# A graph attention and feed-forward kernel: three halves of the first product moved behind a branch, a longer ring of one-hots, and twelve one-hots formed by ScalarE

## The chip, the cores and the metric

The kernel runs on one core of one Trainium2 chip. The metric is device time in microseconds (us) of one execution; all times below are in us unless marked ns. The core's engines work side by side, each through its own queue of instructions in order, and wait for one another by semaphores: TensorE (PE in the profile; its weight loads are PEld), VectorE (DVE), ScalarE (ACT), GpSimd (POOL) and SyncE (SP), which here mostly issues DMAs.

## What is computed

1250 nodes carry 768 features each; 21250 directed edges (source, destination) join them, sorted by destination. The reference, cut to what matters here, is two layers of graph attention, and a feed-forward part with a few routed tokens behind them:

```
def gat_layer(x, W, att_src, att_dst, bias, src, dst, heads, out_ch, concat):
    h = (x @ W.T).reshape(n, heads, out_ch)
    a_src = jnp.einsum('nhc,hc->nh', h, att_src)
    a_dst = jnp.einsum('nhc,hc->nh', h, att_dst)
    e = jax.nn.leaky_relu(a_src[src] + a_dst[dst], NEG_SLOPE)
    m = jax.ops.segment_max(e, dst, num_segments=n)
    ex = jnp.exp(e - m[dst])
    denom = jax.ops.segment_sum(ex, dst, num_segments=n)
    alpha = ex / (denom[dst] + EPS)
    out = jax.ops.segment_sum(alpha[:, :, None] * h[src], dst, num_segments=n)
...
x = x + _L0_gnn_ref(_layernorm(x), edge_index, W1, ..., b2)   # 8 heads of 128, then 1 of 768
x = x + _L0_ffn_ref(_layernorm(x)[None], ...)[0]
```

## The kernel before

The kernel makes the sparse graph dense. Nodes are taken in 10 blocks of 125. A table `ct` holds for each pair (source, destination) how many edges join them; attention then becomes dense arithmetic on tables of 125 sources by 1250 destinations and products on TensorE.

**Counting the edges (to about 101 us).** The edges come in 170 chunks of 125, 17 to a block of destinations. For each chunk, `hot_chunk` (line 263) makes two tables of zeros and ones with one row per edge: `at` (which of a block's 125 sources; `places`, line 258, makes those of eleven chunks at once on VectorE, GpSimd makes those of the other six singly, line 276) and `by`, 420 wide (which of 42 destinations, times 10 blocks of sources). `by` is made by one VectorE instruction, line 241, into one of 12 places of `ring`: it is 1 where the column's number equals the edge's `key`. `count_chunk` (line 284) multiplies the two on TensorE and adds up in PSUM banks, one for each area of 50 destinations, three banks in turn. When an area is complete, ScalarE copies it to `ct` and to `staged` (lines 309 and 314); when a block of destinations is complete, TensorE turns it (line 322) and ScalarE makes `absent` of it (line 323), a table that is huge where no edge is.

**Between and behind the count.** `h1_half` (line 495) computes a half of h for one block of nodes and one of two groups of heads: 6 matmuls in fp32, which the profile records as 12, and a copy from PSUM by ScalarE (line 395). There are 40 such halves, in the list `fill`. Six are put between the chunks of the last three blocks, 20 directly behind the count (line 684), 2 and 4 behind the branch (lines 701 and 708), and the last eight between the steps of heads 0 and 1. `top_of_block` (line 610 in its body) is a VectorE instruction that finds, for one head and one block of destinations, the largest source value among the neighbours. Heads 0 to 3 are done ahead of the branch except for the last block.

**The branch (line 689).** If some edge does not fit its chunk's window, `count_all` counts anew; it is never taken with these inputs. All engines read the number of such edges (line 686) and pass the branch each in its own place: the `issue_after` above it puts the read behind the halves issued so far. Behind it, VectorE finishes the tops of the last block. `load_destination_rows` (line 615) then turns head 0's tops into rows: a small transpose on TensorE (`r_h_p`, line 576), a copy on VectorE, a DMA to DRAM (`r_h_d`) and one back that spreads the rows over all partitions (`rows_h`, line 625).

**The heads.** For each of 8 heads and each of 10 blocks of sources, `weights` forms a table `pt` of 125 by 1250: VectorE (line 634, which needs `rows_h`), ScalarE's exponential (line 637), VectorE again (line 638). TensorE multiplies it with h and adds up in `acc` (line 851). Three `pt` buffers turn. Tops of later heads (line 610), remaining halves, and from head 4 parts of the second layer's product (line 802) stand between the steps. Then follow the second layer (line 1015) and the feed-forward part.

The order on each engine is set by a scheduler at build time, from the order of the source and the `issue_after` hints, so the order of the lines is not that of the queues.

Of the kernel before, what the change touches and what calls it, by code (L numbers as in the profile page):

```python
# [26 lines left out]
BF16 = mybir.dt.bfloat16  # L27
F16 = mybir.dt.float16
I32 = mybir.dt.int32
U16 = mybir.dt.uint16  # L30
AF = mybir.ActivationFunctionType
# [4 lines left out]
D = 768  # L36
# [6 lines left out]
B = 125  # L43
NB = N // B
EC = E // B
# [9 lines left out]
WIN = 42  # L55
SB = N // B
# [16 lines left out]
def gnn_ffn(  # L73
# [25 lines left out]
    nc = tc.nc  # L99

    def pool(name, bufs=1, space=None, stack=ctx):
        if space is None:
            return stack.enter_context(tc.tile_pool(name=name, bufs=bufs, reuse_waits="tile"))
        return stack.enter_context(tc.tile_pool(name=name, bufs=bufs, space=space))
# [28 lines left out]
    ep = pool("early", stack=early)  # L133
# [5 lines left out]
    def ps_count(name):  # L139
        return psum_a.tile([128, 512], F32, tag="count", bufs=3, name=name)  # L140

    src_i = ep.tile([B, EC], I32, name="src_i")
    dst_i = ep.tile([B, EC], I32, name="dst_i")
    nc.sync.dma_start(src_i, src)
    nc.sync.dma_start(dst_i, dst)

    HW = NB * (C1 + 1)
    x4 = big.tile([128, 4 * HW], F32, tag="ga", name="x4")
    x6 = big.tile([128, 4 * HW], F32, tag="gb", name="x6")
    x_in = [x4[:B, b * D : (b + 1) * D] for b in range(4)]  # L150
    x_in += [x6[:B, b * D : (b + 1) * D] for b in range(6)]

# [18 lines left out]
    for i in range(2):  # L171
# [3 lines left out]
    node = ep.tile([B, N], F16, name="node")  # L175
    nc.gpsimd.iota(
        node, pattern=[[1, N]], base=0, channel_multiplier=0, allow_small_or_imprecise_dtypes=True
# [23 lines left out]
    key = ep.tile([B, EC], F32, name="key")  # L201
# [23 lines left out]
    ones = ep.tile([B, 1], F32, name="ones")  # L225
# [14 lines left out]
    def one_hot(t, col, nodes):  # L240
        return nc.vector.tensor_scalar(t, nodes, col, None, op0=OP.is_equal)  # L241
# [1 line left out]

    ring = ep.tile([B, 12, SB * WIN], BF16, name="ring")
    newest = {}

    AT_ONCE = 11
# [2 lines left out]
    def places_at_once(b, r0, r1):  # L252
        n = r1 - r0
        t = ep.tile([B, AT_ONCE, B], BF16, tag="places", bufs=2, name=f"places{b}_{r0}")
        for r in range(r0, r1):
            at_once[b * CPB + r] = t[:, r - r0]
        c = b * CPB + r0
        nc.vector.tensor_tensor(  # L258
            t[:, :n], node[:, :B].unsqueeze(1).to_broadcast([B, n, B]),
            place16[:, c : c + n].unsqueeze(2).to_broadcast([B, n, B]), OP.is_equal,  # L260
        )

    def hot_chunk(c):

        b, r = divmod(c, CPB)
        if r < AT_ONCE and c not in at_once:
            if b > 0:
                places_at_once(b, 0, AT_ONCE)
            else:
                places_at_once(b, r, min(AT_ONCE, r + 6))  # L270
        by = ring[:, c % 12]
        newest["of"] = one_hot(by, key[:, c : c + 1], node[:, : SB * WIN])
        if r < AT_ONCE:
            return at_once[c], by
        at = ep.tile([B, B], BF16, tag="at", bufs=12, name=f"at{c}")
        nc.gpsimd.tensor_scalar(at, node[:, :B], place[:, c : c + 1], None, op0=OP.is_equal)  # L276
        return at, by

# [5 lines left out]
    def count_chunk(c):  # L284
        at, by = hot_chunk(c)
        f = window_of(c)
        for k in areas_of[c]:
            first = k not in banks
            if first:
                banks[k] = ps_count(f"count{k}")  # L290
            d0, d1 = max(f, AREA * k), min(f + WIN, AREA * (k + 1))
            last = c == EC - 1 or k not in areas_of[c + 1]
            newest["count"] = nc.tensor.matmul(  # L293
                banks[k][:B, SB * (d0 - AREA * k) : SB * (d1 - AREA * k)], at,
                by[:, SB * (d0 - f) : SB * (d1 - f)],
                start=first, stop=last, skip_group_check=True,
            )
            if last:
                use_area(k)
# [355 lines left out]
    def first_tops(blocks, hs=range(EARLY)):  # L655
        for b in blocks:
            for h in hs:
                top_of_block(heads[h], b)
# [6 lines left out]
    def fill_behind(what, n):  # L665
        with tc.issue_after(newest[what].ins):
            for _ in range(n):
                fill.pop(0)()

    for b in range(3, NB):  # L670
# [10 lines left out]
            attention_columns()  # L681
            as1_lo, as1_hi = low_high(a1[:, 0], [B, H1, NB], "as1")
        first_tops(behind.get(b, ()), range(4))
    fill_behind("count", 20)
    with tc.issue_after(newest["h1"].ins):
        n_val = nc.values_load(n_i[:1, :1], min_val=0, max_val=E)
    first_tops(range(4, NB - 1), range(4))
# [17 lines left out]
    for h in (4, 5):  # L705
        load_source_row(heads[h], ap, as1_d[h], f"h{h}")
    first_tops(range(4, NB), [4])
    for _ in range(4):
        fill.pop(0)()
    load_source_row(heads[6], ap, as1_d[6], "h6")  # L710
    tops = []
# [293 lines left out]
    for q in range(NB // 2):  # L1005
        pt = pt2[q]
        for i in range(2):
# [14 lines left out]
            for g in (1, 0):  # L1022
                c = slice(g * 384, (g + 1) * 384)
# [4 lines left out]
        c = slice(2 * q, 2 * q + 2)  # L1028
# [158 lines left out]
    for r in range(2):  # L1187
        for g in range(2):
            q = 32 * (2 * (1 - r) + g)
            c = slice(g * 384, (g + 1) * 384)  # L1190
# [67 lines left out]
```

## Time and profile before

| | us |
|---|---|
| median of 3 runs | 757.32 (755.39 to 758.07) |
| the profiled execution | 756.6 |
| its span in the trace | 754.8 |
| TensorE busy | 707.8 (94%) |
| VectorE busy | 555.8 (74%) |
| ScalarE busy | 286.8 (38%) |
| GpSimd busy | 89.5 (12%) |

"Busy" is the time in which an engine executes, without waits that the profile can see; the share is an average over stages with different limits. The page's second part cuts the span into 40 slices of 18.9 us, each digit a busy share in tenths:

```profile
PE   4899899996999877899999999999999999999998
DVE  7969999679999999999999891579686422342313
ACT  5986441114364745655555565004253000010000
```

The first five slices are the count, the next three and a half the halves of h around the branch, then come the heads to slice 25, the second layer to slice 35, and the feed-forward part. VectorE is full from slice 8 to slice 22 and TensorE nearly everywhere; which of the two ends a stage is told by the waits and by the chain that ended last.

### The profile page before, as it was taken

What the parts mean: (1) busy time and instruction counts of PE and PEld (TensorE: products, weight loads), DVE (VectorE), ACT (ScalarE), POOL (GpSimd) and SP (SyncE); (2) the same over time, 40 slices, a digit from 0 to 9 for tenths busy, and PEclk for the clock granted to TensorE, in tenths of its full rate; (3) what the DMA queues carried; (4) which work ended last, traced back from release to release, by engine and by line L of the source; (5) the groups of instructions that cost most, each with busy time, mean ns of one, the idle gap of its engine ahead of it and who ended that gap; (6) DMA issues with size and microseconds to landing.
All of it is one profiled execution on the core that took longest, in us unless ns stands there. A gap on an engine that the chain in (4) does not pass through costs nothing.

```text
span 754.8 us, 10416 instructions
## 1 busy us (share of the span) xinstructions
PE 707.8 (94%) x4136; PEld 541.3 (72%) x4136; DVE 555.8 (74%) x956; ACT 286.8 (38%) x500; POOL 89.5 (12%) x95
## 2 busy tenths in 40 slices
PE   4899899996999877899999999999999999999998
PEld 3767788885999767888887886555555555676755
DVE  7969999679999999999999891579686422342313
ACT  5986441114364745655555565004253000010000
POOL 8357300000000000000000000100011011023110
PEclk9799999997999999999999999999999999999999
DMA  8444000333003220222220200321101010194811
GB/s 229 160 170 172 0 1 1 119 100 106 2 1 104 84 70 1 69 84 70 83 72 1 69 1 24 136 69 38 48 21 42 20 42 20 34 309 132 310 42 42
DMA packets 21702, 58.42 MB, mean 77 GB/s; under 512 B 2414, under 2 KB 7906, under 8 KB 20498
## 3 DMA queue, kind: packets, MB, share of 16 engines
q1 hardware_dynamic: 21598, 57.68, 23.1%
q8 instruction: 33, 0.54, 0.3%
q14 instruction: 19, 0.16, 0.1%
q10 hardware_dynamic: 52, 0.04, 0.0%
HBM read 53.74 MB, written 3.98 MB: 76 GB/s over the span
## 4 chain that ended last, share of the span: by engine, by line
PE 65%; DVE 25%; DMA 4%; issue 4%; ACT 2%; SPq 0%; DVEq 0%; ACTq 0%
PE acc L1015 16%; PE h2p L802 13%; PE acc L851 10%; DVE pt L634 9%; PE h1p L499 8%; DVE pt L638 6%; PE f L1080 5%; PE f L1064 5%; DVE unused L610 5%; DVE ring L241 2%; PE count L293 2%; DMA rows_h<-r_h_d 2%; DMA x<-in_x 2%; PE xt2p L391 1%; DVE st L381 1%
## 5 line engine op out<-in xcount | busy, mean ns | idle before, releaser
L851 PE MATMUL acc<-g,pt 125*125 125x129 f32 x1600 | 191.9, 278 | 23.5 <-DVE pt L638 23.3
L851 PEld LDWEIGHTS acc<-g,pt 125*125 125x125 f32 x1600 | 186.3, 191 | 36.3 <-DVE pt L638 30.8
L637 ACT ACTIVATE pt<-pt,as_lo 125x1250 f32<-125x1250 f32 (+1 forms) x130 | 128.0, 1012 | 174.9 <-DVE pt L634 173.8
L638 DVE SCALAR_TENSOR_TENSOR pt<-pt,ct 125x1250 f32<-125x1250 f32 (+1 forms) x130 | 133.0, 1050 | 5.2 <-ACT pt L637 5.0
L1015 PE MATMUL acc<-h,pt 125*125 125x385 f32 (+1 forms) x400 | 129.7, 486 | 0.0
L634 DVE SCALAR_TENSOR_TENSOR pt<-rows_h,as_hi 125x1250 f32<-125x1250 f32 x80 | 118.9, 1509 | 5.8 <-DMA rows_h<-r_h_d 4.7
L1015 PEld LDWEIGHTS acc<-h,pt 125*125 125x125 f32 x400 | 74.6, 187 | 53.9
L802 PE MATMUL h2p<-w2s,g 128*125 128x384 f32 x320 | 109.0, 488 | 0.1
L499 PE MATMUL h1p<-w1s,xt 128*125 128x256 f32 x480 | 108.5, 382 | 0.5 <-ACT g L395 0.5
L499 PEld LDWEIGHTS h1p<-w1s,xt 128*125 128x125 f32 x480 | 89.3, 189 | 13.6 <-ACT g L395 0.9
L802 PEld LDWEIGHTS h2p<-w2s,g 128*125 128x125 f32 x320 | 57.7, 188 | 36.5 <-issue 0.8
L610 DVE CUSTOM_DVE_ANT_0 unused<-rows,absent 125x1250 bf16<-125x1250 f32 x40 | 58.3, 1458 | 10.0 <-ACTq L689 8.3
L1011 POOL TENSOR_TENSOR xb<-xb,b2r 125x768 f32<-125x768 f32 x10 | 18.3, 1832 | 372.3 <-DMA xb<-in_x 352.3
L610 DVE CUSTOM_DVE_ANT_0 unused<-srow_h,absent 125x1250 bf16<-125x1250 f32 x40 | 58.1, 1453 | 0.3
L276 POOL TENSOR_SCALAR at<-node,place 125x125 bf16<-125x125 f16 x60 | 49.5, 842 | 26.9 <-PE count L293 24.0
L241 DVE TENSOR_SCALAR ring<-node,key 125x420 bf16<-125x420 f16 x170 | 47.8, 344 | 6.3 <-PE count L293 6.2
L1084 DVE TENSOR_TENSOR o<-f,o 125x384 f32<-125x384 f32 x20 | 11.1, 557 | 52.5 <-PE f L1080 28.7
L293 PE MATMUL count<-ring,places 125*125 125x420 bf16 (+26 forms) x192 | 33.5, 303 | 16.0 <-DVE ring L241 15.6
L395 ACT ACTIVATE g<-h1p 125x256 f32<-125x256 f32 x40 | 15.3, 383 | 70.2 <-PE h1p L499 68.6
L293 PEld LDWEIGHTS <-places 125*125 125x125 bf16 x192 | 24.1, 154 | 21.8 <-DVE places L258 9.8
L1080 PE MATMUL f<-wf,gt 128*125 128x384 f32 x120 | 39.5, 486 | 0.0
L1080 PEld LDWEIGHTS f<-wf,gt 128*125 128x125 f32 x120 | 22.5, 188 | 15.1
(189 smaller groups left out, 579.5 us busy)
## 6 DMA issues: line engine op xcount, KB each, us to landing
rows_h<-r_h_d SPq DMA_DIRECT2D x8, 1250.0 KB
w_more<-in_atom_in_t SPq DMA_DIRECT2D x3, 1152.0 KB
w_more<-in_atom_out_t SPq DMA_DIRECT2D x3, 1152.0 KB
x<-in_x SPq DMA_DIRECT2D x10, 336.0 KB
xb<-in_x SPq DMA_DIRECT2D x10, 336.0 KB
srow_h<-as_d SPq DMA_DIRECT2D x5, 625.0 KB
w1n<-in_w SPq DMA_DIRECT2D x2, 1536.0 KB
w1s<-in_w1t SPq DMA_DIRECT2D x2, 1536.0 KB
```

The source lines that it names most:

```text
L241: return nc.vector.tensor_scalar(t, nodes, col, None, op0=OP.is_equal)
L276: nc.gpsimd.tensor_scalar(at, node[:, :B], place[:, c : c + 1], None, op0=OP.is_equal)
L293: newest["count"] = nc.tensor.matmul(banks[k][:B, SB * (d0 - AREA * k) : SB * (d1 - AREA * k)], at, by[:, SB * (d0 - f) : SB * (d1 - f)], ...
L499: newest["h1"] = nc.tensor.matmul(p[:B, :256], xt[:, k, b * B : (b + 1) * B], w1s[g][:, k, i * 256 : (i + 1) * 256], start=(k == 0), stop= ...
L610: nc.vector.tensor_tensor_reduce(out=unused, in0=hd.src_row, in1=absent[:, b], scale=1.0, scalar=-ABSENT, op0=OP.subtract, op1=OP.max, acc ...
L634: begun = nc.vector.scalar_tensor_tensor(o, hd.rows[:, 0, c0:c1], hi, hd.rows[:, 1, c0:c1], op0=OP.add, op1=OP.max)
L637: nc.scalar.activation(o, o, AF.Exp, bias=lo, scale=1.0)
L638: formed = nc.vector.scalar_tensor_tensor(o, o, 1.0, ct[:, s, c0:c1], op0=OP.min, op1=OP.mult)
L802: nc.tensor.matmul(p[:B, :384], groups[i][:, h, b * B : (b + 1) * B], w2h[i][:, h, g * 384 : (g + 1) * 384], start=(h == 0), stop=(h == 3),)
L851: summed = nc.tensor.matmul(acc[g][:B, j * (C1 + 1) : (j + 1) * (C1 + 1)], pt[:, d * B : (d + 1) * B], h1v[h // 4][:, h % 4, s, :], start= ...
L1015: nc.tensor.matmul(acc[g][:B, : c1 - c0], pt[:, s, i * B : (i + 1) * B], h2[:, s, c0:c1], start=(s == 0), stop=(s == NB - 1),)
L1080: nc.tensor.matmul(p[:B, :384], gt[:, m, i, :], wf2[:, m, c], start=(m == 0), stop=(m == KH - 1),)
```

## The change

Five edits, in the order of the diff. The edge indices `src_i` and `dst_i` are no longer tiles of their own but lie in the unused tail of `x6`. `ring` has 15 places in place of 12. In blocks 6 to 9, the `by` tables of chunks 3, 8 and 13 of each block, twelve in all, are formed by ScalarE with two activations: `away` = |key - column|, then max(0, 1 - away), which is 1 where the two are equal and 0 elsewhere, as both are whole numbers. The `at` buffers go from 12 to 10. And `fill_behind("count", 20)` becomes 17, with 7 halves in place of 4 taken from the list behind `load_destination_rows`: the order of the halves in the list stays, so all that are issued from there on are three places earlier in it, and the last eight fall where they did.

```diff
--- before.py
+++ after.py
@@ -139,14 +139,15 @@
     def ps_count(name):
         return psum_a.tile([128, 512], F32, tag="count", bufs=3, name=name)
 
-    src_i = ep.tile([B, EC], I32, name="src_i")
-    dst_i = ep.tile([B, EC], I32, name="dst_i")
-    nc.sync.dma_start(src_i, src)
-    nc.sync.dma_start(dst_i, dst)
 
     HW = NB * (C1 + 1)
     x4 = big.tile([128, 4 * HW], F32, tag="ga", name="x4")
     x6 = big.tile([128, 4 * HW], F32, tag="gb", name="x6")
+    src_i, dst_i = (
+        x6[:B, 6 * D + i * EC : 6 * D + (i + 1) * EC].bitcast(I32) for i in range(2)
+    )
+    nc.sync.dma_start(src_i, src)
+    nc.sync.dma_start(dst_i, dst)
     x_in = [x4[:B, b * D : (b + 1) * D] for b in range(4)]
     x_in += [x6[:B, b * D : (b + 1) * D] for b in range(6)]
 
@@ -243,7 +244,8 @@
 
 
 
-    ring = ep.tile([B, 12, SB * WIN], BF16, name="ring")
+    PLACES = 15
+    ring = ep.tile([B, PLACES, SB * WIN], BF16, name="ring")
     newest = {}
 
     AT_ONCE = 11
@@ -268,11 +270,18 @@
                 places_at_once(b, 0, AT_ONCE)
             else:
                 places_at_once(b, r, min(AT_ONCE, r + 6))
-        by = ring[:, c % 12]
-        newest["of"] = one_hot(by, key[:, c : c + 1], node[:, : SB * WIN])
+        by = ring[:, c % PLACES]
+        if b >= 6 and r in (3, 8, 13):
+            away = ep.tile([B, SB * WIN], F16, tag="away", bufs=1, name=f"away{c}")
+            nc.scalar.activation(
+                away, node[:, : SB * WIN], AF.Abs, bias=key[:, c : c + 1], scale=-1.0
+            )
+            nc.scalar.activation(by, away, AF.Relu, bias=ones, scale=-1.0)
+        else:
+            newest["of"] = one_hot(by, key[:, c : c + 1], node[:, : SB * WIN])
         if r < AT_ONCE:
             return at_once[c], by
-        at = ep.tile([B, B], BF16, tag="at", bufs=12, name=f"at{c}")
+        at = ep.tile([B, B], BF16, tag="at", bufs=10, name=f"at{c}")
         nc.gpsimd.tensor_scalar(at, node[:, :B], place[:, c : c + 1], None, op0=OP.is_equal)
         return at, by
 
@@ -681,7 +690,7 @@
             attention_columns()
             as1_lo, as1_hi = low_high(a1[:, 0], [B, H1, NB], "as1")
         first_tops(behind.get(b, ()), range(4))
-    fill_behind("count", 20)
+    fill_behind("count", 17)
     with tc.issue_after(newest["h1"].ins):
         n_val = nc.values_load(n_i[:1, :1], min_val=0, max_val=E)
     first_tops(range(4, NB - 1), range(4))
@@ -705,7 +714,7 @@
     for h in (4, 5):
         load_source_row(heads[h], ap, as1_d[h], f"h{h}")
     first_tops(range(4, NB), [4])
-    for _ in range(4):
+    for _ in range(7):
         fill.pop(0)()
     load_source_row(heads[6], ap, as1_d[6], "h6")
     tops = []
```

## Prediction

> **What bounds the kernel now.** I read the page's slices, the waits, the chain, then the timeline around the branch and the busy time by stage. First the longest waits of the engines that matter:
>
> ```profile
> DVE unused L610 <- ACTq L689: 8.3, 1, 8.3
> PEld acc L851 <- DVE pt L638: 30.8, 25, 7.3
> DVE ring L241 <- PE count L293: 6.2, 3, 3.7
> ```
>
> VectorE's one long wait in the first half is for ScalarE to get past the branch of line 689. The timeline shows it:
>
> ```profile
> 144.89 0.08 DVE L610 DVE_READ_ACCUMULATOR2_ANT top<- 125x1 f32 x1
> 152.19 0.39 ACT L395 ACTIVATE g<-h1p 125x256 f32<-125x256 f32 x1 [2.20 <-PE h1p L499]
> 153.24 1.46 DVE L610 CUSTOM_DVE_ANT_0 unused<-rows,absent 125x1250 bf16<-125x1250 f32 x1 [8.27 <-ACTq L689]
> 161.37 0.27 PE L576 MATMUL r_h_p<-ident,r_h 125*20 125x125 f32 x1
> 163.39 0.32 SPq L625 DMA_DIRECT2D rows_h<-r_h_d  x1
> 171.02 1.52 DVE L634 SCALAR_TENSOR_TENSOR pt<-rows_h,as_hi 125x1250 f32<-125x1250 f32 x1 [1.51 <-DMA rows_h<-r_h_d]
> 178.20 9.28 PEld L851 LDWEIGHTS acc<-g,pt 125*125 125x125 f32 x60 [7.35 <-DVE pt L638]
> ```
>
> VectorE has its tops done at 144.97. ScalarE copies one half of h after another as TensorE delivers them; after the copy at 152.19 (ends 152.58) it passes the branch, and VectorE goes on at 153.24, 0.66 later. From there one chain runs without slack: four tops, head 0's rows through DRAM, the first pt at 171.02, TensorE's first acc at 178.20 after 7 idle. Now the stages:
>
> ```profile
> 60.00:71.00 11.00, 9.64 (x82) 7.23 (x81) 11.00 (x39) 7.10 (x15) 10.42 (x15) 1.00 0.53 205
> 71.00:82.00 11.00, 10.55 (x61) 8.93 (x60) 11.00 (x24) 4.54 (x10) 5.64 (x7) 0.85 0.01 1
> 82.00:92.00 10.00, 9.40 (x63) 8.09 (x62) 10.00 (x23) 5.10 (x10) 1.44 (x3) 1.00 0.00 0
> 92.00:102.00 10.00, 8.98 (x65) 7.46 (x65) 9.89 (x24) 5.67 (x11) 0.00 (x0) 1.00 0.01 2
> 145.00:153.00 8.00, 8.00 (x39) 6.97 (x38) 0.00 (x0) 1.16 (x3) 0.00 (x0) 1.00 0.21 85
> 280.00:323.00 43.00, 34.59 (x293) 32.53 (x292) 43.00 (x46) 27.49 (x46) 0.00 (x0) 1.00 0.09 31
> ```
>
> (Columns: stretch, its length, PE, PEld, DVE, ACT, POOL busy, clock, DMA share, GB/s.) The count of edges up to 102 is VectorE's (fourth number), TensorE close behind. 145 to 153 is TensorE's alone. 171 to 323 is VectorE's; then the chain of waits passes to TensorE to the end. So microseconds won for VectorE at the branch reach the end, if TensorE keeps pace until 323, where it has room.
>
> **Part 1: three halves of h behind the branch.** The chain has
>
> ```profile
> 101.60 53.16 PE h1p L499 x246
> ```
>
> so one matmul is 53.16 / 246 = 0.216, and a half (12 records) 2.59. In the built order ScalarE's branch stands behind three copies fewer, so it comes 3 x 2.59 = 7.78 earlier. VectorE's cover for this is its 8.27 of idle; had its tops ended later, they would take the rest.
>
> Behind the branch, the same instructions follow: four tops (153.24 to 159.21), the small ones to r_h, 28 matmuls on TensorE before r_h_p (155.22 to 161.37). None is nearer to another limit than before, so the rows also come the same amount earlier. SyncE's order is unchanged: r_h_d, the load for head 5, rows. The 1.5 MB load of w2s begins at 139.24, when the twentieth half ends, and stays there; the stretch 153 to 162 moved 2 GB/s, so it had landed by 153, and the rows, now issued near 155.2, miss it. If they met its last 0.7 MB (85 GB/s for 8), at the 214 GB/s of 162 to 171 they would lose 3.
>
> TensorE then does 80 matmuls behind r_h_p where it did 44: from 161.6 - 8.2 = 153.4, 80 x 0.216 = 17.3, to 170.7. The first pt was whole at 178.20 and will be at 170.0. So acc starts near 170.8 without the idle: the moved halves cost nothing as long as they fill this gap of 7; 0.8 of delay goes against three pt buffers (VectorE comes to its fourth pt only at 182.5 - 8.2). On ScalarE three of the copies now stand between the first exponentials; the exponential of the third pt is done at 170.2 by this count, and VectorE wants it at 171.4. Cost 0.
>
> r_h_p of head 1 now stands behind all seven halves, so its copy is issued only some 8.55 ahead of head 1's first pt, as head 2's was before (234.77 to 243.33, no wait shown). Head 0's needed 170.99 - 161.96 = 9.03. Between 0 and 0.8: I take 0.3 lost.
>
> **Part 2: ring and ScalarE's one-hots.** Removed from VectorE: 12 one-hots. The chain has 11 in 3.20 and 11 in 2.95, 0.28 each: 3.4. Three more places let VectorE form three more in its wait of 3.69 ahead of 53.1: 0.8. If VectorE alone set the count's end, it would come 4.2 earlier.
>
> Added to ScalarE: 24 activations of 420 elements, which the trace lacks. Nearest rows:
>
> ```profile
> L455 ACT ACTIVATE unused<-x,less 125x768 bf16<-125x768 f32 x3 | 2.8, 936 | 0.1
> L454 ACT ACTIVATE less<-total 125x1 f32<-125x1 f32 x3 | 0.6, 203 | 0.1
> ```
>
> The line through both gives 0.203 + 419 x 0.956 ns = 0.60; the second waits for the first, so a chunk is 1.2 and all are 14.5. ScalarE is busy 22.4 of the 42 from 60 to 102: 36.9 with them. In 60 to 71 it is 7.1 + 3.6 = 10.7 of 11: full. And it works in order: the one-hot of chunk 105 stands behind the two copies of the area before, that of 110 behind both `absent`, that of 115 behind a copy that waits for 110's count. So TensorE gets new waits in block 6. Its work from area 14's end (64.7 before, some 64.2 after) to the count's end: 112 count matmuls x 0.12 (19 took 2.28) + 5 x 0.75 of transposes + 1.0 + 5.5 halves x 2.65 = 32.8, which without any wait ends at 97.0; before it ended at 101.4, so with 3.9 of waits. Going through the new orders with these durations I find some 4 of waits: block 6 is 3 to 4 late at its end, then TensorE catches up, since VectorE is ahead by then; it ends near 101.0. Bounds: 4.2 earlier (no waits) and 3.6 later (block 6's three chunks fully on the path). I take 0.4 earlier, as TensorE's own work is the nearest limit.
>
> [...]
>
> The other edits cost nothing. The indices in x6's tail: same two loads at the head of SyncE's queue, and the tile's next owner writes at 44.8 at the earliest; without that cover the first cast (3.58) would move. Ten `at` buffers for twelve: GpSimd forms them a block ahead and idles 5.4 before 77.25; a late one would cost its 0.84.
>
> **Sum.** 7.78 + 0.4 - 0.3 = 7.9 off the profiled execution's 756.6 (span 754.8 and 1.8 around it): 748.7. That execution is 0.7 under the median of 757.32, so 749.3 against the runs shown.
>
> **Rivals.**
> (a) VectorE sets the whole count: end 4.2 earlier, ScalarE at the branch 152.58 - 7.78 - 4.2 = 140.6, VectorE 144.97 - 4.2 = 140.8. Gain 7.8 + 4.2 - 0.3 = 11.7: 745.6. For it: 100% busy from 60 to 92. Against: the halves woven in leave TensorE only 4. Chance 0.17.
> (b) ScalarE drags in block 6 for good: 3.6 later, gain 7.78 - 3.6 - 0.3 = 3.9: 753.4. For it: 10.7 of 11. Against: 4 to 6 idle of each later 10 or 11. Chance 0.08.
> (c) Slower: every one of the 12 pairs lies uncovered before a matmul that needs it, since ScalarE is in order behind waits for TensorE. Count end 14.5 later, branch 14.5 - 7.8 = 6.7 later: 764. It decides from 7.5 / 12 = 0.63 a chunk. Against: those of blocks 7 to 9 stand in the queue well ahead of their use. Chance 0.07.
> (d) The edit doesn't move the branch, because VectorE really waits for TensorE (it passes at 154.75) or a load: only part 2 is left, 0 to 1: 756.8. Against: 153.24 is ahead of TensorE's passing. Chance 0.03.
>
> **How the numbers follow.** The forecast has 0.65: gain 6 to 10, 747 to 751. The range reaches to (a) and (b), with 1 on either side for the scatter of the runs (755.39 to 758.07): 744.5 to 753.8. 0.3% is 2.3, about what a measurement of this kernel tells from no change. Faster by more: forecast, (a) and 0.07 of (b): 0.89. Within: the rest of (b) and (d), 0.04. Slower: (c), 0.07.
>
> **What would show it.** VectorE's wait at the branch falls from 8.3 to about 4 (under 1 is (a)); its first top behind it at 145.1; the first pt at 162.9; acc at 170.8 with no idle of 7 before it; the unbroken run of h1p begins near 101.0; an activation of 420 takes 0.60; chunk 118's count ends 3 to 4 later than 67.1. It is wrong if that run begins past 109, or if TensorE, not VectorE, sets 171 to 323.

## The result and the profile after

The changed kernel takes 749.15 us (median of 4 runs, 747.68 to 749.99), beside 757.7 for the kernel before on the same chip (4 runs, 755.39 to 759.69). The ratio is 0.9886, with a 95% interval from 0.9853 to 0.9919. The profiled execution took 747.68, its span is 745.9 (before 756.6 and 754.8): 8.9 less.

The timeline around the branch, now line 698, in the changed kernel (start, duration, engine, line, operation, in brackets the idle time before it and what ended it):

```profile
139.35 0.08 DVE L619 DVE_READ_ACCUMULATOR2_ANT top<- 125x1 f32 x1
140.96 0.39 ACT L404 ACTIVATE g<-h1p 125x256 f32<-125x256 f32 x1 [2.21 <-PE h1p L508]
141.73 1.46 DVE L619 CUSTOM_DVE_ANT_0 unused<-rows,absent 125x1250 bf16<-125x1250 f32 x1 [2.30 <-ACTq L698]
145.72 7.97 PE L508 MATMUL h1p<-w1s,xt 128*125 128x256 f32 x28 [2.21 <-PEq L698]
153.52 0.27 PE L585 MATMUL r_h_p<-ident,r_h 125*20 125x125 f32 x1
153.83 0.28 DVE L587 COPY r_h_s<-r_h_p 20x125 f32<-20x125 f32 x1 [4.99 <-PE r_h_p L585]
155.54 0.32 SPq L634 DMA_DIRECT2D rows_h<-r_h_d  x1
163.24 1.52 DVE L643 SCALAR_TENSOR_TENSOR pt<-rows_h,as_hi 125x1250 f32<-125x1250 f32 x1 [1.58 <-DMA rows_h<-r_h_d]
170.69 4.48 PEld L860 LDWEIGHTS acc<-g,pt 125*125 125x125 f32 x39
```

VectorE goes on behind the branch 11.51 earlier than before (141.73 against 153.24). But the first pt comes only 7.78 earlier (163.24 against 171.02). The 3.7 between lie in two lines that the kernel before does not have in this form. TensorE idles 2.21 at the branch, ended by its own sequencer (PEq L698), where before it idled 0.48 for a copy; and its 28 matmuls ahead of r_h_p take 7.97 and no longer 6.31. VectorE, which before waited 1.33 for r_h_p, waits 4.99. The idle of 7.35 ahead of acc is gone, as the last line shows: no bracket.

The stages (stretch, its length, busy PE, PEld, DVE, ACT, POOL, clock, DMA share, GB/s), those of the prediction first, and one more of the count:

```profile
60.00:71.00 11.00, 7.57 (x53) 5.82 (x53) 11.00 (x34) 9.51 (x18) 8.46 (x11) 0.88 0.39 157
71.00:82.00 11.00, 10.99 (x78) 9.57 (x77) 11.00 (x27) 9.90 (x21) 9.64 (x10) 0.96 0.01 1
82.00:92.00 10.00, 10.00 (x76) 8.63 (x75) 10.00 (x23) 9.55 (x20) 2.46 (x2) 1.00 0.00 1
92.00:102.00 10.00, 10.00 (x63) 8.54 (x62) 9.76 (x15) 5.67 (x10) 0.00 (x0) 1.00 0.01 2
145.00:153.00 8.00, 7.28 (x26) 6.05 (x27) 3.81 (x16) 0.53 (x2) 0.00 (x0) 0.79 0.01 2
280.00:323.00 43.00, 36.83 (x294) 33.29 (x293) 43.00 (x47) 25.99 (x39) 0.00 (x0) 1.00 0.09 31
64.20:97.97 33.77, 31.28 (x212) 26.61 (x213) 33.63 (x77) 28.75 (x56) 16.36 (x16) 0.95 0.01 4
```

TensorE loses time in block 6 (7.57 busy of 11, before 9.64) and from 71 on has no idle left (30.99 of 31; before 28.93). The four groups of TensorE that idle between 60 and 102 show for whom (busy, mean ns, idle before and what ended it):

```profile
L302 PE MATMUL count<-ring,places 125*125 125x420 bf16 (+27 forms) x78 | 11.3, 285 | 0.4 <-ACT staged L404 0.4
L302 PE MATMUL count<-ring,at 125*125 125x420 bf16 (+22 forms) x44 | 6.8, 292 | 0.2 <-ACT ring L279 0.2
L331 PE MATMUL cp<-ident,staged 125*125 125x125 f16 x50 | 3.9, 224 | 0.3 <-ACT staged L404 0.3
L573 PE MATMUL a1tp<-ident,x 128*125 128x128 f32 (+1 forms) x3 | 1.0, 350 | 2.5 <-DVE a L580 2.5
```

So 2.5 of the 3.4 are waits for VectorE's copies of `a` (`a1tp` is a small transpose from which VectorE takes the attention columns `a`); ScalarE's one-hots account for 0.2. The count ends earlier all the same: the unbroken run of halves of h begins at 97.97, not at 101.44. The mean granted clock of TensorE is 0.79 from 145 to 153 (0.50 from 147 to 150), where before it was 1.00.

ScalarE's new work, as groups of instructions (busy, mean ns, idle before):

```profile
L279 ACT ACTIVATE ring<-away,ones 125x420 bf16<-125x420 f16 x12 | 7.7, 645 | 0.2
L276 ACT ACTIVATE away<-node,key 125x420 f16<-125x420 f16 x11 | 7.1, 646 | 0.2
```

One activation takes 0.645 (one record of the second group is missing in the trace).

### The profile page after: what moved, and what is told of

It reads as the page before. It is cut to its first block, busy times and chain, and to the rows that moved or that the text cites. A ratio compares the mean times of both kernels' runs of the same rounds, so it can differ in the third digit from the quotient of the medians.

```text
span 745.9 us, 10432 instructions
## 1 busy us (share of the span) xinstructions
PE 704.6 (94%) x4136; PEld 538.9 (72%) x4136; DVE 553.1 (74%) x944; ACT 299.5 (40%) x524; POOL 91.0 (12%) x95
## 4 chain that ended last, share of the span: by engine, by line
PE 43%; DVE 28%; issue 4%; DMA 4%; ACT 1%; DVEq 0%; SPq 0%; ACTq 0%
PE acc L1024 16%; DVE pt L643 13%; DVE pt L647 9%; PE h2p L811 9%; PE f L1089 5%; PE f L1073 5%; DVE unused L619 5%; PE acc L860 3%; DMA rows_h<-r_h_d 3%; PE h1p L508 1%; PE xt2p L400 1%; PE candp L1190 1%; DMA r_h_d<-r_h_s 1%; PE a2p L831 1%; PE hidp L1146 1%
## 5 line engine op out<-in xcount | busy, mean ns | idle before, releaser
L860 PE MATMUL acc<-g,pt 125*125 125x129 f32 x1600 | 189.3, 276 | 17.4 <-DVE pt L647 17.3
L860 PEld LDWEIGHTS acc<-g,pt 125*125 125x125 f32 x1600 | 183.9, 189 | 29.8 <-DVE pt L647 24.2
L285 POOL TENSOR_SCALAR at<-node,place 125x125 bf16<-125x125 f16 x60 | 51.1, 868 | 27.2 <-PE count L302 24.8
L242 DVE TENSOR_SCALAR ring<-node,key 125x420 bf16<-125x420 f16 x158 | 45.4, 349 | 5.3 <-PE count L302 5.3
L302 PE MATMUL count<-ring,places 125*125 125x420 bf16 (+25 forms) x192 | 30.6, 300 | 12.5 <-DVE ring L242 11.8
```

The costliest lines, as they stand in the source:

```text
L302: newest["count"] = nc.tensor.matmul(banks[k][:B, SB * (d0 - AREA * k) : SB * (d1 - AREA * k)], at, by[:, SB * (d0 - f) : SB * (d1 - f)], ...
L860: summed = nc.tensor.matmul(acc[g][:B, j * (C1 + 1) : (j + 1) * (C1 + 1)], pt[:, d * B : (d + 1) * B], h1v[h // 4][:, h % 4, s, :], start= ...
```

## The experiments

What had to be explained is TensorE's stop at the branch. Theory 1, as a guess to be tried: it waits for its code behind the branch, which comes over the DMA engines that, in the changed kernel, are just then busy with w2s. That load is issued when the twentieth half of h is done, at 135.77 (before: 139.24), and its data and the next source row keep the 16 DMA engines busy until 143.7 (a share of 0.94 from 137 to 143.5); the branch now comes right into it. The DMA queues between 142 and 144 (packets, MB, share of 16 engines) show packets of data and of instructions in the same stretch (q1 carries data, q8 and q14 instructions; which of the 16 engines moved a packet is not shown):

```profile
q1 hardware_dynamic: 104, 0.43, 54.4%
q8 instruction: 1, 0.02, 2.9%
q14 instruction: 1, 0.01, 1.0%
```

Rival 2: the jump costs TensorE this time in any case.

### E1: the load of w2s later

```diff
-        nc.sync.dma_start(to, row.partition_broadcast(128))
+        hd.load = nc.sync.dma_start(to, row.partition_broadcast(128))
...
-    load_w2(0)
+    with tc.issue_after(heads[6].load.ins):
+        load_w2(0)
```

> The changed kernel, but the load of the first half of the second weights (w2s, 1.5 MB) is issued behind the seventh head's source row, some 27 us behind the branch, and no longer ahead of it. Theory 1 (TensorE's jump to its code behind the branch waits for that code, which comes by the same DMA engines as the 1.5 MB): TensorE idles 0.5 us or less at the branch, not 2.21; its 28 matmuls ahead of r_h_p take 6.3 us at full clock, not 7.97 at 0.79; first pt near 159.9, not 163.24; 745.7 us. Rival 2 (the jump itself costs TensorE this, whatever the DMA does): the 2.2 us stay, and the time stays at 749.

745.99 us (744.58 to 746.32), ratio 0.9845 [0.9823, 0.9866]. w2s is issued at 163.35. The timeline of this kernel:

```profile
144.13 6.31 PE L508 MATMUL h1p<-w1s,xt 128*125 128x256 f32 x28 [0.47 <-ACT g L404]
150.28 0.27 PE L585 MATMUL r_h_p<-ident,r_h 125*20 125x125 f32 x1
160.05 1.52 DVE L643 SCALAR_TENSOR_TENSOR pt<-rows_h,as_hi 125x1250 f32<-125x1250 f32 x1 [1.64 <-DMA rows_h<-r_h_d]
```

The stop and the slow matmuls behind it are gone; TensorE waits only 0.47, for a copy, and its 28 matmuls take 6.31. r_h_p comes 3.24 earlier than in the changed kernel: 1.59 by the stop and 1.66 by the 28 matmuls. The place of the load decides here, as theory 1 has it; rival 2 is not borne out. The jump itself can be read from the view of one source line (instruction, duration three times as minimum, median, maximum in ns, start). First the changed kernel, then E1, then the kernel before:

```profile
L698 PEldq COMPARE_BRANCH  x1: 5324/5324/5324, 140.1 to 140.1; - x1
L698 PEldq EVENT_SEMAPHORE  x1: 51/51/51, 145.5 to 145.5; - x1
```

```profile
L698 PEldq COMPARE_BRANCH  x1: 3347/3347/3347, 140.2 to 140.2; - x1
```

```profile
L689 PEldq COMPARE_BRANCH  x1: 367/367/367, 151.3 to 151.3; - x1
```

TensorE's sequencer takes the branch ahead of the end of the matmuls before it: at 140.1 where the last of them ends at 143.5 in the changed kernel, at 140.2 and 143.7 in E1, at 151.3 and 154.7 before, 3.4 to 3.5 in all three. Behind the jump of 0.37 TensorE idles 0.48, behind the one of 3.35 0.47, both for a copy, and behind the one of 5.32 it idles 2.21. The two kernels take the jump at the same time; their first instruction packet on q8 shows at 143.0 in the changed kernel and at 141.2 in E1. The packet comes 1.8 later with the data in flight, and the jump is 1.98 longer. No view names the engine that a packet is for; that q8 is TensorE's is inferred from this agreement.

### E2: part 1 alone

```diff
-    fill_behind("count", 20)
+    fill_behind("count", 17)
...
-    for _ in range(4):
+    for _ in range(7):
```

> The kernel before with 17 and 7 halves, not 20 and 4; its one-hots and its ring stay as they were. Part 1 by the prediction's own step: 7.8 less 0.3, so 750.1 us, and the first pt 7.5 earlier than 171.02. Theory 1: w2s is issued near 139.2 as before, the branch comes 7.8 earlier and meets it; TensorE idles some 2 us there and the 28 matmuls behind take near 8 us, so first pt near 167 and 753.5 us. Rival 2: the same stall, so this run alone does not tell 1 from 2.

751.47 us (749.51 to 753.06), 0.9917 [0.9896, 0.9939], first pt at 163.81. The time lies between the two numbers expected. The first pt is near the 163.5 of the prediction's step only because the count ended 1.24 earlier in this profile (halves from 100.20, before 101.44). The stop is there, but the 28 matmuls behind it take 6.31, as in the kernel before, and not the 8 us that were expected:

```profile
148.02 4.15 PE L499 MATMUL h1p<-w1s,xt 128*125 128x256 f32 x18 [2.27 <-DVE top L610]
148.02 3.96 PEld L499 LDWEIGHTS h1p<-w1s,xt 128*125 128x125 f32 x19 [2.68 <-issue]
```

These matmuls need nothing of the tops; the page names whatever event came last, and the weight load beside it shows "issue", that is no wait that the profile knows. The jump took 0.35 here, but the q8 packet came at 145.6, as the load of w2s ended, and TensorE went on 2.42 after it (2.72 in the changed kernel). So a stop of 2.27 was seen behind a jump of 0.35 as well.

### E4: part 1 alone, w2s later

Both edits, E1's and E2's, in the kernel before.

> Part 1 alone as in the run with 17 and 7 halves in the kernel before, and w2s issued behind the seventh head's source row. Theory 1: no idle of over 0.5 us at the branch, clock 1.00 behind it, first pt near 163.5, 750.0 us: the step as the prediction had it. Rival 2: 753.5 us, as without the later load.

748.76 us (746.90 to 750.10), 0.9878 [0.9854, 0.9902]. Idle at the branch 0.62, 28 matmuls in 6.31, first pt 164.61 in the profiled execution, whose count happened to end late (102.61, against 100.20 in E2's). 2.7 less than E2 by the medians; the intervals of the ratios overlap a little, so the size is loose, the direction that of theory 1. Counted from the begin of the halves, the first pt comes after 62.00, in the kernel before after 69.58: 7.58 less.

### E8: the load meets the branch in the kernel before

```diff
+    fill.insert(22, fill.pop(19))
```

> The kernel before, its halves in another order: the 20th half of the list is formed three places later, so that w2s, which takes the memory of the weights which that half is the last to read, is issued near 147.0 and not 139.24, while the branch stays where it is (152.6). Theory 1: TensorE now idles some 2 us at the branch and runs at a lower clock behind it; up to 3.4 us slower, 761 us. Rival 2: nothing changes, 757.6 us.

758.06 us (756.00 to 759.07), 0.9997 [0.9983, 1.0011]: no change, and theory 1 as stated is wrong here. w2s was issued at 148.43 and its data moved until 156.2, right across the branch, and yet:

```profile
156.64 6.31 PE L499 MATMUL h1p<-w1s,xt 128*125 128x256 f32 x28 [0.47 <-ACT g L395]
```

The q8 packet can explain it: it came at 147.9, ahead of the data and 4.8 ahead of the jump. A load across the branch is not enough; what fits is that the packet, too, must fall into it.

### E3: part 2 alone

The changed kernel with 20 and 4 halves.

> The changed kernel with 20 and 4 halves as before, so that only the longer ring and ScalarE's twelve one-hots are left of the change. Theory 1: TensorE's unbroken run of halves begins near 98.0, as in the changed kernel, against 100.2 to 102.9 in the four profiles in which VectorE forms all one-hots; the load of w2s is over some 5 us ahead of the branch, so there is no idle over 0.5 us there; some 3.6 us faster than before, 754.3 by the medians. The prediction's step for this part: 0.4 us, 757.5.

754.86 us (754.54 to 756.95), 0.9972 [0.9959, 0.9986]: 2.8 less than before. The halves begin at 98.33:

```profile
98.33 26.98 PE L508 MATMUL h1p<-w1s,xt 128*125 128x256 f32 x124
```

TensorE idles 0.48 at the branch; the packet (143.4) does fall into the load, but the jump comes only at 148.2, 4.8 behind it. First pt 168.04: 3.0 earlier than before. Parts 1 and 2 add up when nothing stops TensorE: 9.3 (E4, 758.1 less 748.76) and 2.8 (757.7 less 754.86) give 12.1, and E1 measured 12.1 (758.1 less 745.99).

### E5 and E6: what in part 2 counts

E5 lets VectorE form all one-hots; E6 takes the ring back to 12 places and `at` to 12 buffers.

```diff
-        if b >= 6 and r in (3, 8, 13):
+        if False:
```

```diff
-    PLACES = 15
+    PLACES = 12
...
-        at = ep.tile([B, B], BF16, tag="at", bufs=10, name=f"at{c}")
+        at = ep.tile([B, B], BF16, tag="at", bufs=12, name=f"at{c}")
```

> The changed kernel with all one-hots formed by VectorE; the ring of 15 places and the 10 buffers of at stay. Theory 1 (part 2's gain is VectorE's 3.4 us of one-hots that ScalarE takes over): the run of halves begins at 100 to 102.5, and the time is that of part 1 alone, 751.5. Rival 2 (the gain is the longer ring's): it begins near 98, and the time stays at 749.

> The changed kernel with a ring of 12 places and 12 buffers of at as before; ScalarE still forms its twelve one-hots. Theory 1: the three places bring 0.8 us at most, so the run of halves begins at 98 to 99 and the time is 749 to 750. Rival 2 (the gain is the longer ring's): it begins past 100, and the time is near 751.5.

E5: 749.83 us (749.40 to 750.22), 0.9903 [0.9876, 0.9930]. E6: 748.10 us (747.37 to 749.05), 0.9879 [0.9852, 0.9907]. These times do not tell the rivals apart; the begin of the halves does better, E5 first, then E6:

```profile
100.59 24.61 PE L508 MATMUL h1p<-w1s,xt 128*125 128x256 f32 x113
```

```profile
99.84 25.47 PE L508 MATMUL h1p<-w1s,xt 128*125 128x256 f32 x117
```

The four profiles with a ring of 12 and VectorE alone have 101.44, 100.20, 102.61 and 102.85; a ring of 15 alone (E5) lies among them. ScalarE's share with a ring of 12 gives 99.84; the eight profiles of this study with both edits have 97.97 to 99.43, 98.5 in the mean. Read so, most (1.9 of 3.3 in the means) is ScalarE's work, and the places may bring some 1.3 on top of it, where 0.8 was expected; with one profile each of E5 and E6 this is an indication and not shown. In the time of the whole, the longer ring shows no gain (E6 748.10, the changed kernel 749.15).

### E7: w2s later, 15 and 9 halves

```diff
-    fill_behind("count", 17)
+    fill_behind("count", 15)
...
-    for _ in range(7):
+    for _ in range(9):
```

> The changed kernel with w2s issued behind the seventh head's source row and two halves more moved behind the branch (15 and 9). Theory 1: VectorE's 2.02 us of wait at the branch and its 1.60 us for r_h_p behind it go, since TensorE's and ScalarE's last halves ahead of the branch come 5.2 us earlier; the first pt comes 3 to 3.6 us earlier than 160.05, and 742.5 to 743.5 us. Rival 2 (TensorE has become the bound behind the branch): its two halves more there put the first acc off, VectorE waits for a pt buffer, and the time stays at 746.

742.54 us (741.63 to 743.46), 0.9808 [0.9785, 0.9832], as theory 1 had it, first pt at 157.00:

```profile
140.63 6.28 PE L508 MATMUL h1p<-w1s,xt 128*125 128x256 f32 x28 [1.20 <-DVEq L698]
147.39 0.27 PE L585 MATMUL r_h_p<-ident,r_h 125*20 125x125 f32 x1 [0.48 <-DVE r_h L631]
```

Now TensorE waits for VectorE at both places: the tops ahead of the branch are the bound.

### E9 to E12: how far this goes

E9: 16 and 8, load ahead of the branch. E10: 13 and 11, load later. E11: 16 and 8, load later. E12: 15 and 9, load ahead of the branch.

> The changed kernel with 16 and 8 halves in place of 17 and 7, and w2s where it was, ahead of the branch. Theory 1: TensorE is done with its work ahead of the branch 2.6 us earlier (near 140.9), but the packet with its code still comes only as the load of w2s ends (near 143), so it goes on at 145.5 to 146 as before, now after an idle of 4.5 to 5 us; r_h_p near 153.5, first pt near 163, 748.5 to 749.5 us: the half moved brings nothing. Rival 2 (the jump costs TensorE a fixed 2.2 us): idle 2.2, r_h_p 2.6 earlier, 746.6 us.

E9: 751.97 us (749.74 to 753.15), 0.9932 [0.9908, 0.9955]. Neither expectation held:

```profile
142.85 6.31 PE L508 MATMUL h1p<-w1s,xt 128*125 128x256 f32 x28 [0.48 <-ACT g L404]
```

The packet came in the load (142.7) and TensorE did not stop at all. The first pt came at 158.62, 4.6 earlier than in the changed kernel, and still the whole was slower.

> The changed kernel with w2s issued behind the seventh head's source row and 13 and 11 halves. With 15 and 9 VectorE waited 0.26 us at the branch and r_h_p waited for VectorE, so the tops ahead of the branch are what is left on the path: two halves more moved bring 0 to 0.5 us there, 742 to 742.5 us. Rival: TensorE's halves behind the branch now delay the weighted sums so that VectorE waits for a pt buffer, and the time goes up to 743 to 746.

E10: 755.50 us (751.52 to 759.80), 0.9977 [0.9954, 1.0001]. The rival was right in kind and too small: VectorE waits 11.3 for acc between 165 and 365. TensorE had idled 6.46 at the branch, for VectorE, and has two halves more behind it than in E7: its first acc comes at 175.53, in E7 at 169.94.

> 16 and 8 halves as in the run before last, and w2s issued behind the seventh head's source row. If the load cost nothing at the branch in that run (its idle there was 0.48 us and r_h_p came at 149.0), r_h_p comes within 0.7 us of 149.0 here; if the load still delayed TensorE's jump, r_h_p comes 1 us or more earlier, VectorE being the next bound. And if that run lost its gain between 200 and 350 us by the order of work that 16 and 8 halves bring, VectorE waits for acc some 7 us there again and the time is 750 to 752; if it was the load's place that brought this, 743 to 745.

E11: 750.93 us (750.19 to 752.36), 0.9921 [0.9896, 0.9945]. r_h_p at 147.66, 1.34 ahead of E9's 149.0; but the run of halves began 1.34 earlier too (98.09 against 99.43), so the load had cost E9 nothing at the branch. And the loss behind it is that of 16 and 8 halves, wherever the load stands. What VectorE waited for from 165 to 365 (us in total, times, longest), in E1, E9 and E11:

```profile
DVE pt L643 <- PE acc L861: 1.1, 2, 0.9
```

```profile
DVE pt L643 <- PE acc L860: 7.7, 11, 1.5
```

```profile
DVE pt L643 <- PE acc L861: 7.5, 11, 1.4
```

In E11 these begin behind one line of TensorE's timeline:

```profile
249.44 4.05 PE L861 MATMUL acc<-g,pt 125*125 125x129 f32 x20 [3.31 <-DVE pt L647]
```

TensorE had idled 3.31 for VectorE's weights, and 20 matmuls that take 2.37 and 2.47 in the two groups of 20 from 258.26 and 262.43 took 4.05; then VectorE waits for them in turn. Why the order of work that 16 and 8 bring does this and that of 15 and 9 does not was not tried. The traces do show that TensorE's longest single wait for weights between 165 and 365 goes with it: 1.8 in E7, 2.5 in E1, 3.3 in E9 and E11, 4.6 in E10, beside waits of VectorE for acc of 0, 1.1, 7.7, 7.5 and 11.3 in all.

> 15 and 9 halves with w2s ahead of the branch, the counterpart of the fastest kernel so far, in which the first instruction packet at the branch came at 137.1 and TensorE could go on at 139.5. Theory 1: here the packet waits for the load of w2s and comes at 141 to 144; TensorE goes on some 2.4 later, at 143.5 to 146.5, after an idle of 4 to 7 us; first pt 3 to 6 us later than 157.0, and 746 to 749 us. Rival (as with 16 and 8: TensorE has the code that it needs already, whatever the packet does): idle as in its counterpart, 1.2 us, first pt near 157, 742.5 us.

E12: 743.07 us (741.10 to 743.63), 0.9806 [0.9783, 0.9829]: no loss, as in its counterpart E7. The packet came at 137.1, just ahead of the data (from 137.9).

All fourteen kernels by the place of that packet (us; "load" is the stretch from w2s's issue to the last data behind it; the packet is the first one on q8 around the branch):

| kernel | halves | load | jump at, takes | packet | TensorE on, idle before | 28 matmuls | first pt |
|---|---|---|---|---|---|---|---|
| before | 20, 4 | 139.2 to 146.8 | 151.3, 0.37 | 146.7 | 155.22, 0.48 | 6.31 | 171.02 |
| E8 | 20, 4 | 148.4 to 156.2 | 152.7, 0.37 | 147.9 | 156.64, 0.47 | 6.31 | 172.57 |
| E3 | 20, 4 | 136.1 to 144.3 | 148.2, 0.37 | 143.4 | 152.12, 0.48 | 6.31 | 168.04 |
| after | 17, 7 | 135.8 to 143.7 | 140.1, 5.32 | 143.0 | 145.72, 2.21 | 7.97 | 163.24 |
| E6 | 17, 7 | 137.7 to 145.4 | 142.0, 5.39 | 144.9 | 147.66, 2.27 | 7.96 | 164.60 |
| E2 | 17, 7 | 138.0 to 146.0 | 142.3, 0.35 | 145.6 | 148.02, 2.27 | 6.31 | 163.81 |
| E5 | 17, 7 | 138.4 to 146.0 | 142.7, 0.35 | 145.6 | 147.99, 1.86 | 8.00 | 165.12 |
| E1 | 17, 7 | later | 140.2, 3.35 | 141.2 | 144.13, 0.47 | 6.31 | 160.05 |
| E4 | 17, 7 | later | 144.7, 0.36 | 146.3 | 148.78, 0.62 | 6.31 | 164.61 |
| E9 | 16, 8 | 137.2 to 146.1 | 138.9, 0.35 | 142.7 | 142.85, 0.48 | 6.31 | 158.62 |
| E11 | 16, 8 | later | 137.6, 0.35 | 139.1 | 141.51, 0.48 | 6.31 | 157.38 |
| E12 | 15, 9 | 136.9 to 145.2 | 136.1, 0.36 | 137.1 | 140.61, 1.11 | 6.28 | 156.95 |
| E7 | 15, 9 | later | 136.0, 0.35 | 137.1 | 140.63, 1.20 | 6.28 | 157.00 |
| E10 | 13, 11 | later | 129.8, 0.35 | 130.9 | 139.74, 6.46 | 7.36 (24 in the trace) | 156.49 |

With 20 and 4 halves the packet comes 4.6 to 4.8 ahead of the jump, wherever the load stands; with 17 and 7 it comes behind the jump, by 1.0 to 1.6 with the load later and by 2.9 to 3.3 with the load across it. So moving the halves did two things: it brought the branch into the load, and it changed when the packet comes. Why it did the second is not shown.

With 17 and 7 halves TensorE goes on 2.4 to 2.8 after the packet in all four kernels in which it falls into the load, and in those four alone there is a stop that neither a copy nor VectorE's arrival at the branch explains. In E9 it falls into the load and nothing stops (idle 0.48, for a copy); why is not shown. That the load causes the stop is shown by E1 against the changed kernel, with the same work on TensorE, and again by E4 against E2; that it does so by holding up the code is the author's reading of the packets and the jumps, which no view shows. What sets E9 apart from the four stays open.

## Why the prediction was right in its total, and where it was wrong

The total was 749.3 against 749.15, but two of its steps were off by some 3 us each, in opposite senses: that the total came out so near was luck.

**Part 1, the branch.** Three halves of 2.59 moved: ScalarE's last copy ahead of the branch ends at 141.35, not 152.58. Of these 11.23 the earlier end of the count has 3.47, and the rest is 7.76, where the step had 7.78. From the begin of the halves to the first pt, part 1 without the stop brings 7.58 (E4) and 7.64 (E1). The step was right up to the first pt; by the medians E4 gains 9.3 in the whole, and where the rest arises was not traced. Right, too, is the filled gap: acc at 170.69 without the idle, predicted 170.8.

**Part 1, behind the branch: the step that failed.** "Behind the branch, the same instructions follow ... None is nearer to another limit than before." TensorE was, at its branch. The prediction did look at the load of w2s, but only asked whether it meets the rows ("it had landed by 153, and the rows ... miss it"), and it had it stay at 139.24 when part 2, which brings the twentieth half forward, brings the load forward with it. What met the load was TensorE's jump, in part 1 alone as well (E2). It cost 2.01 at the branch (TensorE goes on 9.50 earlier where VectorE goes on 11.51 earlier) and 1.66 in the 28 matmuls, and VectorE's wait for r_h_p of 4.99 is its face on the other engine. Without the meeting (E1) the kernel takes 745.99, so the meeting cost 3.2. That is near the 745.6 of rival (a), which had a chance of 0.17.

TensorE's jumps took 3.35 (E1), 5.32 (the changed kernel) and 5.39 (E6), in the eleven other kernels 0.35 to 0.37. E1 and the changed kernel differ only in when w2s is issued, and with its data in flight the jump took 1.98 more. What makes a jump take 3.35 and not 0.35 is not shown. The prediction had weighed no such cost.

**Part 2, mis-sized.** The prediction took 0.4, between bounds of 4.2 earlier and 3.6 later; measured were 3.5 in the profile, and 2.8 in the whole by E3. Its own sum was 32.8 of TensorE's work from 64.2 on, and 4 of waits; the trace has 31.28 and 2.49 (64.20 to 97.97), which is the 3.0 that it was off. The idle in block 6 has the size foreseen (3.43 of the 11 from 60 to 71, before 1.36), but not its cause. The one-hots of ScalarE, which were to cause it, made TensorE wait 0.2; two waits of 2.10 and 0.39 are for VectorE's copies of `a`, and 0.7 is for ScalarE's copies to `staged`, which its one-hots may have delayed. ScalarE was busy 9.51 of the 11, not 10.7. An activation took 0.645, not 0.60, and was hidden. Behind block 6 nothing was left of the 2.07 that TensorE had idled before. Rival (a), VectorE setting the whole count, was nearly true for the count, which ended 3.47 earlier where (a) has 4.2. The move to ScalarE paid, since before it VectorE was busy 41.9 of the 42 from 60 to 102 and ScalarE 22.4. What leaving the twelve one-hots with VectorE would cost is read from E6 against E2, which differ in the twelve one-hots and in where the indices lie: ratios of 0.9879 and 0.9917, some 2.9, with intervals that overlap a little.

**Head 1's rows** were to lose 0.3. No wait of VectorE for them is seen. From 171 to 323 VectorE idles 0.66 where it had idled 1.58. The end is 8.9 earlier in the profiled executions, against 7.78 at the first pt.

**The signs that were named.** VectorE's wait at the branch: 2.30 (4 expected, under 1 for rival (a)); first top behind it 141.73 (145.1); first pt 163.24 (162.9); acc 170.69 (170.8); halves from 97.97 (101.0); the last count of block 6 ends at 70.4, 3.3 later than before (3 to 4). The first pt and acc are as near as they are because the two errors meet there. The last count of block 6 came as named for another reason, as said above. The halves and the first top stand ahead of TensorE's stop and show part 2's error alone, 3.0 and 3.4. A sign between the two, such as the time of r_h_p, was not among those named.

Rivals (b), (c) and (d) did not occur: nothing ran past 101.4, no pair lay open, and the branch moved.

## What to carry to other kernels

Ahead of a branch, look at what the DMA engines do while it is taken: instruction packets pass then too (q8, 0.02 MB between 142 and 144), and a load of 1.5 MB issued 4.3 before TensorE's jump cost 3.2 here, by way of an engine that has nothing to do with it. A total that comes out right proves no step of a prediction; compare times at each place on the chain, and who is waited for, since here one gain that was 3.1 larger than forecast and one loss of 3.7 that was not forecast made one right sum, and the idle of block 6 had the right size for a wrong reason. And moving one slice of work at a time is not monotone: 17 and 7, 16 and 8, 15 and 9, 13 and 11 halves with the load later took 745.99, 750.93, 742.54 and 755.50.

## What the runs showed of the hardware that was not expected

- Instruction packets of about 16 KB have a queue of their own (q8: 33 packets, 0.54 MB in the changed kernel). The one at the branch came 1.8 later with w2s in flight (143.0 in the changed kernel, 141.2 in E1). TensorE's sequencer went on 2.5 after it in both (145.5 and 143.7); in E9 TensorE's matmuls began 0.15 after it (142.85 and 142.7).
- TensorE's sequencer took the branch 3.4 to 3.5 ahead of the end of the matmuls before it (before, after, E1), and a jump of 3.35 did not show: behind it TensorE idles 0.47 in E1, for a copy, as it idles 0.48 behind the one of 0.37 in the kernel before.
- Behind an idle of 2.21 the granted clock in the changed kernel was 0.98 from 145.7 to 147, 0.50 from 147 to 150 and 0.94 from 150 to 153. Behind stops of 2.21, 1.86 and 2.27 (after, E5, E6) the 28 matmuls took 7.96 to 8.00, behind one of 2.27 (E2) they took 6.31. So the length of the stop alone did not decide it; what did is not shown.
